# Stores of normalized rows moved from SyncE's to ScalarE's DMA queue, and two parameter loads moved to a later block

## The chip, the cores and the metric

The kernel runs on one core of a Trainium2 chip. The metric is the time of one execution on the device in microseconds (us), as the median of several runs. Engines are named as in the profile: PE is TensorE's matmul (PEld its weight load), DVE is VectorE, ACT is ScalarE, POOL is GpSimd, and SP is SyncE, which here only issues DMAs.

## The reference

Two layers work on x (2708 rows of 256 floats) and a 0/1 adjacency matrix of 2708 x 2708. Each layer is attention and then a mixture of experts, each on a layer-normalized input and each added back to x:

```python
x = x + _L0_gnn_ref(_layernorm(x), adj, L0_gnn_W, L0_gnn_a)
x = x + _L0_ffn_ref(_layernorm(x)[None], L0_ffn_Wg, ...)[0]
x = x + _L1_gnn_ref(_layernorm(x), adj, 1, L1_gnn_W_gcn, ...)
x = x + _L1_ffn_ref(_layernorm(x)[None], L1_ffn_gate_w, ...)[0]
```

The change lies in layer 1. Its attention is a softmax over neighbours, `h_prime = att @ h`, then elu, a projection and maps with logarithms and hyperbolic functions, row by row. Its experts (16 of them, two per row) are:

```python
topk_vals, topk_idx = jax.lax.top_k(x @ gate_w + gate_b, 2)
topk_w = jax.nn.softmax(topk_vals, axis=-1)
h = jax.nn.relu(jnp.einsum('bsh,ehf->bsef', x, w1) + b1)      # F = 512
expert_out = jnp.einsum('bsef,efh->bseh', h, w2) + b2
moe = sum over the two chosen experts of topk_w * expert_out
y = x + moe                        # x is the normalized row here
return (y - mean(y)) / sqrt(var(y) + eps) * gamma + beta
```

The normalized row thus has three uses: it is routed, it is the input of its experts, and it is the start value of y.

## The kernel before, in words

**Tiles and stages.** The 2708 rows are 22 tiles: 20 of 128 rows and two of 74. Layer 0 ends at about 670 us. In layer 1 the attention sums run from about 735 to 871 us: 44 matmuls a tile at L1772, from masks that POOL (L1620) and ACT (L1622) widen. When a tile's sum is done, `finish1` (L1975 to L2002) applies elu on ACT and DVE. When a part of tiles is finished (parts are tiles 0-3, 4-5, 6-9, 10-11, 12-15, 16-17, 18-19, 20-21), `points1` (L2029 to L2111) follows: a DVE and ACT chain of small operations, then for each tile the residual sum with x_d (DVE, L2090; the rows come by `fetch_row`, L1633, on SP), the statistics, and finally for each tile `apply_s` on ACT (L2106, the instruction itself is L506), which writes the normalized row to a tile `xr`. Right behind it `experts1.store` (L2107, the DMA is at L1020) writes this row to `sums[0]` in memory as the start value of y. A tile of 74 rows is stored in two pieces, so there are 24 stores.

**Routing.** Two tiles at a time, `logits1` turns the rows on PE (L515), copies them out on ACT (L610, L613), multiplies with the gate on PE (L520) and takes the logits on DVE (L626). For a group of tiles (0-5, 6-11, 12-17, 18-21), `route1` picks the two best experts (DVE, L648 to L667), ranks rows within experts on PE (L680 to L690), numbers them on DVE (L710 to L746), and POOL scatters the rows to `rows_d`, sorted by expert (L753, two indirect DMAs a tile). After groups 1, 2 and 3 `plan` (L862 to L952) decides which expert each block of 128 sorted rows has: PE L908 (`number_ps`), PE L921 (`where_ps`), ACT L925 (`where`, read by SP into registers at L827), DVE L933, L935 and L937, PE L943 (`bias_ps`), ACT L948. After group 1 (tiles 6-11, counted from 0) blocks 0 to 7 are planned, after group 2 blocks 8 to 19, after group 3 the rest. In the text below "group 2" and "rank 2" belong to tiles 12-17, "group 3" and "rank 3" to tiles 18-21.

**Blocks.** For each of the 45 blocks SP loads both weights of its expert (L834 `w1`, L838 `w2`, 512 KB each) into one of four rooms, so block b waits for the room of block b - 4, and fetches the 128 rows (L850). PE turns them (L515, called turn(b) below), ACT copies them out (L1108), PE multiplies with `w1` (L972, 16 matmuls, hid(b)), ACT applies relu (L976, four), PE multiplies with `w2` (L987 and L990, out(b)), DVE scales (L994, L996), and POOL adds the result to `sums` in memory (L1001). After the last block the sums are read back (L1528), normalized, and stored (L2238).

**What sets the order.** The order of instructions on PE, ACT, DVE and SP is the order in which the program records them (`manual_schedule`, L176). It is recorded by a planner, `Clock` (L65 to L121): each piece of work is a generator that yields an engine and an estimated time before each operation, or a mark it has to wait for; the planner always goes on with the piece that can start first on its modelled engines. An estimate that changes therefore shifts the order of all later operations on all four engines. DMAs of SP are not entered in the planner as work of an engine.

**Gamma and beta.** `late_pools` (L2160 to L2172, called at L1945 once the attention is nearly recorded) makes the buffers of the expert stage and loads gamma and beta with two broadcasting DMAs of SP (`broadcast_rows`, L230). Beta is first read by `add_to_x`, from block 20 on. `beside(b)` (L2174) starts side work at given blocks.

Of the kernel before, what the change touches and what calls it, by code (L numbers as in the profile page):

```python
# [22 lines left out]
P = 128  # L23
# [124 lines left out]
def kernel(  # L148
# [25 lines left out]
    nc = tc.nc  # L174

    ctx.enter_context(tc.manual_schedule(engines={ET.PE, ET.Activation, ET.DVE, ET.SP}))  # L176
    N, D = x.shape
# [50 lines left out]
    def broadcast_rows(name, src, offset, n, queue=nc.gpsimd, pool=const):  # L228
        tl = pool.tile([P, n], F32, name=name)
        queue.dma_start(  # L230
            tl, bass.AP(tensor=src.tensor, offset=src.offset + offset, ap=[[0, P], [1, n]])
        )
        return tl
# [32 lines left out]
    def xr0_tile():  # L266
        return lasting.tile([P, RW], F32, name="xr", bufs=5)
# [14 lines left out]
    def parts_of_rows(r):  # L282

        return [(0, r)] if r == P else [(0, 64), (64, r)]
# [78 lines left out]
    def stat(n, dtype=F32):  # L363

        count[0] += 1
        cols, bufs = next(of for of in STATS if n <= of[0])
        return sm.tile([P, cols], dtype, name=f"stat{count[0]}", tag=f"stat{cols}",
                       bufs=bufs)[:, :n]
# [45 lines left out]
    def rsqrt_steps(v, o=None):  # L414

        yield SMALL
        shifted = ts(v.bitcast(I32), 1, OP.logical_shift_right, dtype=I32)
        yield SMALL
        y = ts(shifted, -1.0, OP.mult, float(0x5F3759DF), OP.add, dtype=I32).bitcast(F32)
        yield SMALL  # L420
        r = tt(v, y, OP.mult)
        yield SMALL
        r = tt(r, y, OP.mult)
        yield SMALL
        h = sts(r, -10.0 / 3.0, OP.add, r, OP.mult)
        yield SMALL
        y = sts(h, 5.0, OP.add, y, OP.mult)
        c = 0.375
        yield SMALL
        h = sts(v, -0.5 * c ** 3, OP.mult, y, OP.mult)  # L430
        yield SMALL
        h = tt(h, y, OP.mult)
        yield SMALL
        return sts(h, 1.5 * c, OP.add, y, OP.mult, o)
# [361 lines left out]
    class Experts:  # L796
# [217 lines left out]
            self.sum_hidden(b, ht, ps)  # L1014
            self.add(b, self.scaled(b, ps, w))

        def store(self, t, r, src):

            for lo, hi in parts_of_rows(r):
                ins = nc.sync.dma_start(self.sums[0][t * P + lo:t * P + hi, :], src[lo:hi])  # L1020
                for _, other in self.adds[0]:
                    tc.declare_no_dep(ins.ins, other, reason="other tokens' rows")

# [604 lines left out]
    def xr_tile():  # L1628
        return side.tile([P, RW], F32, name="xr1", bufs=13)

    def fetch_row(tl, src, t, r):
        for lo, hi in parts_of_rows(r):
            nc.sync.dma_start(tl[lo:hi], src[t * P + lo:t * P + hi, :])  # L1633
# [167 lines left out]
    last = pairs[AHEAD - 1]  # L1801
# [44 lines left out]
    for part in range(2):  # L1846
        for t in range(FIRST + part, LAST, 2):
            for i in range(2):
# [6 lines left out]
    router1 = Router(1, E1, groups1, wg1, bg1, side)  # L1855
    router1.fill()
    sums1 = [sums_d(f"sums1_{k}", zero=k == 1) for k in range(2)]
    experts1 = Experts(1, router1, L1_ffn_w1, L1_ffn_b1, L1_ffn_w2, AF.Relu, sums1,
                       ("wide", "wide", "acc"), lambda b: xr_tile(),
                       lambda: side.tile([P, D], F32, name="lo", bufs=2).rearrange(  # L1860
                           "p (c n) -> p c n", n=P),
                       lambda: w1x[:, 1, :], SURE1, DEEP)
# [166 lines left out]
    def points1(part):  # L2029

        lo, n = part[0][0], len(part)
        hi = lo + n
        xq, xp_slots, x_at = [], [], [Mark() for _ in range(n // 2)]

        def fetch_x():
            for k in range(0, n, 2):
                xp_slots.append((yield from xps.get()))
                for t, r in part[k:k + 2]:
                    xq.append(xr0_tile())
                    fetch_row(xq[-1][:, :D], x_d, t, r)  # L2040
                clock.moved(x_at[k // 2], 0.9, 2.0)

        sq = emb_sq[:, lo:hi]
        v = stat(2 * n)
        yield SMALL
        nc.vector.tensor_scalar(v[:, :n], sq, MIN_NORM * MIN_NORM, None, op0=OP.max)
        yield SMALL
        nc.vector.tensor_scalar(v[:, n:], sq, 1.0, None, op0=OP.add)
        y = yield from rsqrt_steps(v)
        yield SMALL  # L2050
        roots = tt(v, y, OP.mult)
        yield SMALL
        u = tt(roots[:, :n], roots[:, n:], OP.add)
        log = yield from half_log(u)
        yield SMALL
        clock.start(fetch_x())
        inward = sts(log, 0.5 * LEAST, OP.max, y[:, :n], OP.mult)

        for q, (t, r) in enumerate(part):
            yield "ACT", 0.5  # L2060
            nc.scalar.activation(emb[:r, t, 1:], emb[:r, t, 1:], AF.Tanh, scale=inward[:r, q:q + 1])
            yield "ACT", 0.7
            nc.scalar.activation(square[:r, 1:], emb[:r, t, 1:], AF.Square,
                                 scale=0.5, bias=half[:r], accum_out=sig_sq[:r, t:t + 1])

        y = yield from rsqrt_steps(sig_sq[:, lo:hi])
        yield SMALL
        s_n, e = tt(sig_sq[:, lo:hi], y, OP.mult), stat(n)
        yield "ACT", 0.22
        nc.scalar.activation(e, s_n, AF.Exp)  # L2070
        yield SMALL
        ie = recip(e)
        yield SMALL
        sinh = tt(e, ie, OP.subtract)
        by = common[:, lo:hi]
        yield SMALL
        nc.vector.scalar_tensor_tensor(by, sinh, 0.25, y, op0=OP.mult, op1=OP.mult)
        yield SMALL
        cosh = tt(e, ie, OP.add)
        yield SMALL  # L2080
        ratio = recip(by)
        yield SMALL
        ratio = sts(cosh, 0.5, OP.mult, ratio, OP.mult)
        yield SMALL
        nc.vector.tensor_scalar(emb[:, lo:hi, 0], ratio, -1.0, None, op0=OP.add)
        for q, (t, r) in enumerate(part):
            if q % 2 == 0:
                yield x_at[q // 2]
            yield "DVE", 0.5
            nc.vector.scalar_tensor_tensor(x1[:r, t, :], emb[:r, t, :], by[:r, q:q + 1], xq[q][:r, :D],  # L2090
                                           op0=OP.mult, op1=OP.add)
            yield "DVE", 0.62
            ln_f1.stats(x1[:r, t, :], t, r)
            if q % 2:
                clock.set(xp_slots[q // 2])
        dev = ln_f1.rstd[:, lo:hi]
        yield SMALL
        var = ts(ln_f1.mv[:, lo:hi, 1], LN_EPS, OP.add)
        yield from rsqrt_steps(var, dev)
        yield SMALL  # L2100
        shift = ln_f1.shift(part)
        for q, (t, r) in enumerate(part):
            xr_slots[t] = yield from xrs.get()
            router1.rows[t] = xr_tile()
            yield "ACT", 0.6
            ln_f1.apply_s(router1.rows[t][:r, :D], x1[:r, t, :], t, r, shift[:, q:q + 1])  # L2106
            experts1.store(t, r, router1.rows[t][:r, :D])  # L2107
            if q % 2:
                clock.start(logits1(part[q - 1:q + 1], taken_at[t - 1]), urgency(part))
        if hi == group_of(part)[-1][0] + 1:  # L2110
            clock.start(route1(group_of(part)), urgency(part))  # L2111
# [46 lines left out]
    experts1_scope, last = ExitStack(), {}  # L2158

    def late_pools():  # L2160
        last["pool"] = ctx.enter_context(tc.tile_pool(name="gamma_beta", bufs=1))
        for name, src in (("gamma", L1_ffn_gamma), ("beta", L1_ffn_beta)):
            last[name] = broadcast_rows(name, src, 0, D, nc.sync, last["pool"])
        experts1.pool = experts1_scope.enter_context(tc.tile_pool(name="experts1", bufs=1))
        room = experts1.pool.tile([P, 4 * D * 2], F32, name="room2")
        experts1.add_room(2, room[:, :1024], room[:, 1024:])
        for k in range(3, DEEP):
            room = mask_flat.bitcast(F32)[:, 2 * T * D + (k - 3) * 2048:][:, :2048]
            experts1.add_room(k, room[:, :1024], room[:, 1024:])
        last["numbers"] = experts1.pool.tile([P, (T - LATE) * P], F32, name="numbers")  # L2170
        last["marks"] = experts1.pool.tile([P, KEEP, (T - LATE) * P], F32R, name="marks")
        last["kept"] = experts1.pool.tile([P, KEEP, 2, D], F32R, name="kept")  # L2172

    def beside(b):  # L2174
        if b == 10:
            clock.start(number_rows(), 3)
        if 20 <= b < 20 + T:
            clock.start(add_to_x(*tiles[b - 20]), 3)

# [22 lines left out]
    def number_rows():  # L2202
        yield "POOL", 2.0
        nc.gpsimd.iota(last["numbers"], pattern=[[1, (T - LATE) * P]], base=LATE * P,
                       channel_multiplier=0, allow_small_or_imprecise_dtypes=True)
# [295 lines left out]
```

## Time and profile before

| what | value |
|---|---|
| median of 3 runs | 1139.43 us (1137.65 to 1140.55) |
| the profiled execution's own time | 1135.28 us |
| its span, first to last instruction | 1133.6 us |
| mean granted clock of TensorE | 0.961 |
| PE busy | 1038.0 us, 92% of the span |
| DVE, ACT, POOL busy | 48%, 51%, 33% |
| L506 in layer 1, one | 0.585 us |
| L1020 in layer 1: 24 issues on SP, one | 0.319 to 0.547 us, median 0.322 |
| gamma and beta (L230) on SP | at 871.28 and 871.68, 0.35 and 0.42 us |

Times in the profile count from the span's start. A group's row gives its line, engine, operation, output tile and input tiles; a bracket behind a row of the timeline gives the idle time of the engine before it and what released it. The name "SPq" stands for SP's queue of instructions that issue DMAs. "issue" and "remote" as releaser mean that the engine waited for nothing that the profile shows. The busy share is also given in 40 equal slices of the span, one digit each, in tenths.

### The profile page before, as it was taken

How to read it: one execution, taken by the hardware profiler on the slowest of the kernel's cores; microseconds unless marked ns; L12 is line 12 of the kernel's file. 1: busy time of each engine (PE TensorE's matmuls, PEld its weight loads, DVE VectorE, ACT ScalarE, POOL GpSimd, SP SyncE). 2: the span in 40 equal slices, each digit the busy share in tenths (PEclk: the TensorE clock that was granted, in tenths of full speed). 3: DMA queues.
4: the chain of work that ended last, by engine and by line, in shares of the span. 5: the costliest groups of instructions: out<-in, count | busy, mean ns of one | idle time of the engine just before them, and what ended most of it. 6: DMA issues, size and time to landing. Idle time of an engine off the chain costs nothing. (4 is left out here: it accounts for less than half of the span.)

```text
span 1133.6 us, 21472 instructions
## 1 busy us (share of the span) xinstructions
PE 1038.0 (92%) x6707; PEld 921.6 (81%) x6707; DVE 542.4 (48%) x2210; ACT 576.4 (51%) x1602; POOL 368.5 (33%) x425
## 2 busy tenths in 40 slices
PE   5999999998989999999999999898985967999994
PEld 3788888887879999998999854898984856999882
DVE  7778888887421111101110347577865553122257
ACT  4866667664524444444444346545653633544454
POOL 7531112111242222112213361352534155434350
PEclk9999999999999999999999999997996788999997
DMA  9965454431889999999899959401114656785893
GB/s 289 282 248 177 137 176 152 170 95 55 306 252 283 331 323 321 325 305 319 257 312 331 356 155 279 160 1 51 53 61 130 179 138 144 162 203 105 227 292 129
DMA packets 161862, 234.38 MB, mean 207 GB/s; under 512 B 10891, under 2 KB 137798, under 8 KB 159032
## 3 DMA queue, kind: packets, MB, share of 16 engines
q1 hardware_dynamic: 143356, 209.90, 57.0%
q0 software_dynamic: 18384, 23.03, 10.6%
q8 instruction: 56, 0.92, 0.3%
q14 instruction: 66, 0.54, 0.2%
HBM read 205.54 MB, written 54.59 MB: 229 GB/s over the span
## 5 line engine op out<-in xcount | busy, mean ns | idle before, releaser
L996 DVE TENSOR_SCALAR yo<-out_ps,w 128x256 f32<-128x256 f32 x89 | 43.0, 483 | 383.3 <-PE out_ps L990 376.2
L1346 PE MATMUL att_ps<-g_all,z 128*128 128x257 f32 (+3 forms) x968 | 223.6, 383 | 0.0
L1346 PEld LDWEIGHTS att_ps<-g_all,z 128*128 128x128 f32 (+3 forms) x968 | 174.9, 186 | 29.5 <-issue 2.9
L990 PE MATMUL out_ps<-room,ht 128*128 128x256 f32 x840 | 191.4, 380 | 0.0
L972 PEld LDWEIGHTS hid_ps<-xt,room 128*128 128x128 f32 x1504 | 176.9, 194 | 9.3 <-issue 3.7
L972 PE MATMUL hid_ps<-xt,room 128*128 128x128 f32 x1504 | 178.9, 278 | 5.4 <-issue 2.7
L990 PEld LDWEIGHTS out_ps<-room,ht 128*128 128x128 f32 x840 | 155.5, 191 | 20.0
L1332 ACT ACTIVATE zr<-e_bc,minus_one,g_all 128x256 f32<-128x256 f32 (+3 forms) x242 | 130.2, 591 | 44.4 <-DVE z L1335 44.3
L1772 PE MATMUL att_ps<-half,wide_mask 128*128 128x258 f32 (+1 forms) x962 | 131.3, 295 | 14.9 <-issue 8.1
L976 ACT ACTIVATE ht<-hid_ps,w_t 128x128 f32<-128x128 f32 x376 | 128.6, 364 | 30.3 <-PE hid_ps L972 11.7
L1001 POOL DMA_INDIRECT sums<-yo,xg x43 | 66.8, 1554 | 233.8 <-DVE side L964 188.5
L1772 PEld LDWEIGHTS att_ps<-half,wide_mask 128*128 128x128 f32 (+1 forms) x962 | 124.5, 198 | 19.0 <-issue 14.8
L753 POOL DMA_INDIRECT rows_d<-xr,place x88 | 91.8, 1043 | 119.7 <-DVE xr L497 66.4
L1335 DVE SCALAR_TENSOR_TENSOR z<-zr,mask_t 128x256 f32<-128x256 f32 (+3 forms) x242 | 97.8, 424 | 31.1 <-ACT zr L1332 17.4
L976 ACT ACTIVATE ht<-hid_ps,w1x 128x128 f32<-128x128 f32 x180 | 65.1, 366 | 83.5 <-PE hid_ps L972 67.5
L1001 POOL DMA_INDIRECT sums<-yo,xr x42 | 65.7, 1564 | 117.0 <-DMA sums<-yo,xr 40.6
L966 ACT ACTIVATE w<-xg,side 128x1 f32<-128x1 f32 x43 | 12.7, 294 | 165.8 <-DVE side L964 165.8
L1620 POOL CAST wide_mask<-mask_t 128x1408 fp32r<-128x1408 fp8e4 x34 | 47.0, 1387 | 95.8 <-PE att_ps L1772 95.8
L972 PE MATMUL hid_ps<-lo,wide_mask 128*128 128x128 f32 x368 | 51.2, 297 | 3.5 <-ACT lo L1108 3.0
L972 PEld LDWEIGHTS hid_ps<-lo,wide_mask 128*128 128x128 f32 x368 | 49.5, 211 | 5.7 <-ACT lo L1108 3.9
L515 PE MATMUL tr_ps<-ident,xr 128*128 128x128 f32 (+1 forms) x214 | 39.6, 297 | 14.6 <-ACT xr L506 12.9
L515 PEld LDWEIGHTS tr_ps<-ident,xr 128*128 128x128 f32 (+1 forms) x214 | 28.1, 154 | 22.1 <-ACT xr L506 14.2
(334 smaller groups left out, 1442.6 us busy)
## 6 DMA issues: line engine op xcount, KB each, us to landing
room<-in_L_ffn_W_dram SPq DMA_DIRECT2D x94, 1024.0 KB
room<-in_adj_dram SPq DMA_DIRECT2D x20, 1354.0 KB
wide_mask<-in_L_ffn_w_dram SPq DMA_DIRECT2D x46, 512.0 KB
room<-in_L_ffn_w_dram SPq DMA_DIRECT2D x22, 512.0 KB
mask_t<-in_L_ffn_w_dram SPq DMA_DIRECT2D x22, 512.0 KB
rows_d<-nobody SPq DMA_DIRECT2D x1, 7511.0 KB
rows_d<-nobody SPq DMA_DIRECT2D x5, 1295.0 KB
sums<-nobody SPq DMA_DIRECT2D x2, 2944.0 KB
```

The source lines that it names most:

```text
L515: nc.tensor.transpose(ps[:, c, :r], src[:, c * P:(c + 1) * P], ident[:r, :r])
L753: ins = nc.gpsimd.indirect_dma_start(out=self.rows_d[:, :], in_=self.rows[t][:r], in_offset=None, out_offset=bass.IndirectOffsetOnAxis(ap= ...
L972: nc.tensor.matmul(ps[:, :P], w1_b[:, c, f * P:(f + 1) * P], xt[:, c, :], start=(c == 0), stop=(c == DC - 1))
L976: nc.scalar.activation(ht[:, f, :], ps[:, :P], self.func, bias=self.bias[:, f, b:b + 1])
L990: nc.tensor.matmul(ps[:, :D], ht[:, f, :], self.rooms[b % self.deep][1][:, f, :], start=False, stop=(f == self.FC - 1))
L996: nc.vector.tensor_scalar(yo, ps[:, :D], w, None, op0=OP.mult)
L1001: ins = nc.gpsimd.indirect_dma_start(out=self.sums[k][:, :], in_=yo, in_offset=None, out_offset=bass.IndirectOffsetOnAxis(ap=self.rows.pop ...
L1332: nc.scalar.activation(zr[:k, :n], e_bc[:k, lo:lo + n], AF.Relu, bias=minus_one[:k], scale=g_all[:k, j, D + 1:D + 2])
L1335: nc.vector.scalar_tensor_tensor(z[:k, :n], zr[:k, :n], 1.0, mask_t[:k, j // 2, lo:lo + n, j % 2], op0=OP.add, op1=OP.mult)
L1346: nc.tensor.matmul(accs[i][:r, :D + 1], z[:k, q * P:q * P + r], g_all[:k, j, :D + 1], start=(j == 0), stop=(j == LAST))
L1620: nc.gpsimd.tensor_copy(m, src)
L1772: nc.tensor.matmul(accs[i][:, :D + 2], last_masks[i][:k] if late else wide_masks[i, j % 2][:k, j // 2, :], half_k[:k, j, :], start=(j == 0 ...
```

## The change

`store` takes the issuing engine as an argument, with SP as the default, which layer 0 keeps. In `points1`, layer 1's stores are issued by ACT, directly behind the L506 that makes the row, and the planner is told of 0.4 us of ACT for each. The loads of gamma and beta go from `late_pools` to `beside(10)`; the planner records this call while block 10's work is being recorded, and SP stays their issuer.

```diff
-        def store(self, t, r, src):
+        def store(self, t, r, src, queue=nc.sync):
 
             for lo, hi in parts_of_rows(r):
-                ins = nc.sync.dma_start(self.sums[0][t * P + lo:t * P + hi, :], src[lo:hi])
+                ins = queue.dma_start(self.sums[0][t * P + lo:t * P + hi, :], src[lo:hi])
                 for _, other in self.adds[0]:
...
             yield "ACT", 0.6
             ln_f1.apply_s(router1.rows[t][:r, :D], x1[:r, t, :], t, r, shift[:, q:q + 1])
-            experts1.store(t, r, router1.rows[t][:r, :D])
+            yield "ACT", 0.4
+            experts1.store(t, r, router1.rows[t][:r, :D], nc.scalar)
             if q % 2:
                 clock.start(logits1(part[q - 1:q + 1], taken_at[t - 1]), urgency(part))
...
     def late_pools():
         last["pool"] = ctx.enter_context(tc.tile_pool(name="gamma_beta", bufs=1))
-        for name, src in (("gamma", L1_ffn_gamma), ("beta", L1_ffn_beta)):
-            last[name] = broadcast_rows(name, src, 0, D, nc.sync, last["pool"])
...
     def beside(b):
         if b == 10:
             clock.start(number_rows(), 3)
+            for name, src in (("gamma", L1_ffn_gamma), ("beta", L1_ffn_beta)):
+                last[name] = broadcast_rows(name, src, 0, D, nc.sync, last["pool"])
```

## The prediction

> **What bounds the kernel now.** I read the page first, then busy time by stretches, then waits and timelines of the stretch that stood out. By the page TensorE is the bound, with one hole:
>
> ```profile
> PE 1038.0 (92%) x6707; PEld 921.6 (81%) x6707; DVE 542.4 (48%) x2210; ACT 576.4 (51%) x1602; POOL 368.5 (33%) x425
> PE   5999999998989999999999999898985967999994
> PEclk9999999999999999999999999997996788999997
> ```
>
> Slices of 28 us: the hole is where PE shows 5, 9, 6 and the clock 7, 9, 9, 6. Stretches of layer 1 (us, then busy us of PE, PEld, DVE, ACT, POOL, clock, DMA share, GB/s):
>
> ```profile
> 735.00:871.00 136.00, 119.41 (x927) 116.42 (x926) 93.59 (x440) 72.08 (x188) 58.95 (x60) 0.90 0.17 54
> 871.00:960.00 89.00, 62.99 (x407) 56.23 (x405) 48.78 (x305) 34.88 (x111) 36.31 (x39) 0.79 0.60 154
> 960.00:1070.00 110.00, 109.68 (x767) 103.07 (x768) 25.69 (x101) 53.49 (x175) 45.19 (x29) 1.00 0.70 161
> ```
>
> Attention ends at 871; from 960 on PE is full, with 3.84 us a block, and the end follows it. In between PE is idle for 26 of 89 us. Only there can this change win much. PE's idle time there, from its timeline (start, us, what, idle before and its releaser):
>
> ```profile
> 879.78 2.16 PE L515 MATMUL tr_ps<-ident,xr 128*128 128x128 f32 x8 [8.53 <-ACT xr L506]
> 884.67 0.66 PE L515 MATMUL tr_ps<-ident,xr 128*128 128x128 f32 x2 [1.05 <-DVE stat L391]
> ...
> 913.09 0.20 PE L908 MATMUL number_ps<-fresh_bf,tri 58*58 58x32 bf16 x1 [1.66 <-DVE yo L996]
> ...
> 926.35 1.88 PE L943 MATMUL bias_ps<-hot_f,w1x 16*128 16x12 f32 x8 [8.33 <-issue]
> ...
> 943.95 0.27 PE L680 MATMUL rank_ps<-hot,tri 128*128 128x128 bf16 x1 [3.57 <-DVE hot L667]
> ```
>
> SP's own waits from 780 on (total, times, longest) show what the stores cost it:
>
> ```profile
> SPq L1020 <- ACT xr L506: 26.0, 6, 10.7
> SPq L827 <- ACT where L925: 24.4, 2, 22.4
> ```
>
> The stores make SP wait 26.0 us, yet few of these reach PE: no x_d consumer (L2090) waits for its load, and the one visible case is 1.05 us at 884.67, where block 0's turn needs rows whose fetch stood behind two stores (SP: stores 879.75, fetches 881.68).
>
> **What the Trainium skill says.** "DMA: Bandwidth & Descriptors", section Issuing engines are not separate DMA queues: all issuers end on the same 16 DMA engines; issuing from several saves only sequencer time. So no transfer gets faster here. The trace has no DMA issued by ACT to check this. "Perfetto Trace Analysis", section DMA Instruction — HWDGE: the semaphore wait is on the issuing sequencer. SP's 26.0 us agree. "TensorE: Matmul & The Clock Gate", Part 1: half clock after an idle window of about 3.4 us, full again after about as long busy. It agrees: 16 hid matmuls took 3.76 us at clock 0.50 after the 8.53 us hole, 1.95 us at full clock.
>
> **The change, part by part.** *Gamma and beta* leave SP at 871.28 (0.35 + 0.42 us) for a place between two weight loads of about block 13, in the PE-bound stretch: block 1's weights come 0.8 us sooner, and nothing waits for them at that point. Later, 0.8 us of SP lies beside a 3.84 us block; without that cover it would cost 0.8. I take 0.
>
> *SP* loses 24 issues of 0.32 to 0.40 us, 8 to 10 us in all, and the 26.0 us of waiting. Worth on the path: the 1.05 us at 884.67.
>
> *ACT* gains 24 issues. No row of an ACT issue exists; the nearest is SP's L1020, 0.319/0.322/0.547 us. Each also waits until its own L506 (0.585 us) is done, where before four of these ran in 2.07 us, 0.52 apart. Bounds: 0.32 us a store below, 1.0 above; I take 0.55. In the attention stretch 12 stores are 6.6 us beside an ACT busy 72 of 136: hidden, except in the first group. There the fourth L506 ends 1.65 us later (776.17 + 2.08 + 1.65 = 779.9, where PE turned tiles 2 and 3 at 779.09), while six attention matmuls now stand ahead of the first turn and fill 0.8 us of the 4.41 us hole there. Net 0. For tiles 12 to 15 three stores lie between the 8.53 us hole and the last turn: 3 x 0.55 = 1.65 us on the path. (ACT rounds: 0.96 to 3.0.)
>
> *Order.* The recorded order also moves, because a piece of 0.4 us on ACT enters the planner. By the built program PE now turns block 0 before gating tiles 12 to 15; turns and gates tiles 16, 17 directly after hid(0); ranks group 2 after out(0), hid(2) and turn(3), not after out(2); reads where (L925) on ACT ahead of L506 of tiles 18 and 19; and puts bias before most of hid(5), not after hid(6) and out(4). Rank 3 moves from ahead of hid(8) to behind out(8). Worth:
> - hid(0): last turn ends about 883.4, turn(0) 883.8, L1108 after the L610s at 885.0, hid(0) at 885.5 instead of 886.69: the 1.65 us are more than paid by the 1.05 us and by the gates that now stand beside L1108. Gain 1.2.
> - Stage two: rank 2 from 904.67 to about 901.3 (gate of tiles 16, 17 about 3 us sooner). From rank to number is a DVE chain of 8.4 us: number 909.7. Number to where_ps takes 2.9 us, then ACT and DVE about 2 (before: 5.6 us from where_ps to L925, behind L2070 and L506): bias 914.6, 11.7 us sooner. But hid(5), hid(6), out(4) and turns, 6.2 us, are then still owed: equal work at 920.8, 5.5 us ahead; this contains the 1.2.
> - Against it: hot_of was ready at 922.09 and bias began at 926.35; ACT shows 2.19 and 3.94 us "remote" there. Such hesitations without a visible releaser, 6.5 us at this place (4.3 + 2.2), come at the end of each run of 12 scatters (L753: 807 to 824, 852 to 867, 910 to 927). The change keeps the scatters. Recurring in full, they leave 5.5 - 6.5 = -1.0; absent, they also save a second half-clock spell (out 3.62 instead of 1.89, bias 1.88 instead of 1.08: 2.5), 8.0. I take 3.5, the middle.
> - Stage three: out(5) ended at 932.5, hid(8) began at 945.82: 13.3 us, 3.57 of it waiting for rank 3. The new order has no rank there, but a new wait.
>
> *The new wait.* In the built program SP's and ACT's DMAs take one of eight completion semaphores in turn, and each waits for the DMA eight places before it, whichever engine issued that. The first 20 tiles' stores meet only DMAs that are long done: x_d loads that lead L506 by a whole chain, earlier stores, weights of blocks 0, 4 and 5. But tile 20 waits for both weights of block 9, the second of which waits for out(5); tile 21 waits for w2 of block 10, loaded after out(6), and for the fetch of block 8, issued after that. Queued behind them on ACT: two L613 (0.29 us), L1108 of block 8; waiting for these: gate(20, 21) and hid(8), so PE. Price: from out(6)'s end, w2 issue 0.4, fetch issue 1.0 (four in 4.07 us on SP), landing about 2.5 (estimate: w2 of block 1 issued 873.61, four fetches from 881.68 with turn(0) at 884.67, so at most 3.0), L613 and L1108 1.0, gate 0.65: 5.6. PE has out(7) and turns, 2.7 us, so about 2.9 us idle in place of 3.57. Out(6) ends 4 us after out(5): hid(8) at out(5) + 9.6 to 10.5; 2.9 us sooner, less the rank work (1.3) still owed, less 0.6 for number's later cover: 1.0. Bounds: landing 2 to 8 us, so +2 to -4.
>
> **Sum.** 3.5 + 1.0 + 0 = 4.5 us. The profiled execution took 1135.28 (span 1133.6 and 1.7 around it): it would take 1130.8. It was 4.15 below the median of 1139.43; the prediction is for the median: 1134.9.
>
> **Rivals.** *No change:* the hesitation recurs in full, -1.0, and stage three gives its 1.0: 1139.4. For it: three of three scatter runs end in one. Against: PE's waits there were partly ACT's order, which is changed. The same time would result if ACT's issues were too costly to let the chain move, so that the change only shifts work from SP to ACT. *Larger gain:* no hesitation, 8.0, and stage three 1.6 (number's cover holds): 9.6, so 1129.8. *Slower:* ACT stands at the stores of tiles 20 and 21. If w2(10) lands late, because weights of blocks 9 and 10, five fetches and the residual stores share the DMA engines (share 0.69 at 940 to 950), each us is a us of PE. With the hesitation recurring the gain is gone from a landing of about 3.5 us, and at 8 us the loss is 4, with the half clock for hid(8) (3.78 instead of 1.95, as before): 1143.5. Against: 512 KB at the 266 GB/s seen at 890 to 900 are 2 us.
>
> **How the numbers follow.** Forecast (1133 to 1137) 0.47, of which 0.38 lie below the bound of 0.3% (3.4 us), about what a measurement of this kernel can tell from no change; larger gain 0.20, no change 0.21, slower 0.12. Faster 0.58, same 0.30, slower 0.12. The range leaves out part of the larger gain and most of slower: 1129.5 to 1141.5; the likeliest case's own is 1133 to 1137.
>
> **What would show it.** ACT issues of 0.3 to 0.6 us at L1020; no SP wait at L1020 in layer 1; hid(0) by 885.5; rank 2 near 901; bias between 914 and 921; no stall at rank 3 but one of about 3 us before gate(20, 21), released by ACT L613; the 3.84 us steps begin 4 to 5 us sooner. It is wrong if ACT issues cost over 1 us, if a hesitation stands elsewhere in 900 to 930 with full length, or if the stall ahead of hid(8) passes 6 us.

## The result, and the profile after

The changed kernel takes 1150.1 us (median of 6 runs, 1147.47 to 1152.34) against 1140.6 us for the kernel before on the same chip (1137.65 to 1143.71): a ratio of 1.0088, with a 95% interval of 1.0065 to 1.0112. Run again on another chip, beside a second trace of the kernel before, it is 1.0114 (1.0095 to 1.0133). The forecast of 1134.9 us had the wrong sign, and 1150.1 lies above its range.

From the page of the changed kernel (span 1148.7 us), the lines that answer to those shown of before:

```profile
PE 1046.6 (91%) x6707; PEld 928.7 (81%) x6707; DVE 548.0 (48%) x2210; ACT 578.3 (50%) x1602; POOL 368.1 (32%) x425
PE   5999999999989999999999999997785868999993
PEclk9999999999999999999999999998886779999997
```

The hole is wider, the full-clock slices come back later, and PE is busy for longer (1046.6 us against 1038.0) though its instructions are the same 6707, at a mean clock of 0.957 against 0.961. The three stretches of before, in the changed kernel (us, then busy us of PE, PEld, DVE, ACT, POOL, clock, DMA share, GB/s):

```profile
735.00:871.00 136.00, 119.45 (x925) 116.57 (x926) 97.27 (x436) 72.86 (x185) 55.35 (x57) 0.91 0.14 43
871.00:960.00 89.00, 61.55 (x356) 54.78 (x356) 45.79 (x274) 35.23 (x107) 30.71 (x32) 0.76 0.53 147
960.00:1070.00 110.00, 107.59 (x753) 100.42 (x753) 29.37 (x132) 50.66 (x166) 49.42 (x38) 0.98 0.66 149
```

The attention now ends at 881.6, not at 871, so that in the middle stretch PE gets through 356 matmuls where it had 407. Its idle time there, from its timeline, shows what became of the stalls that were forecast to shrink:

```profile
888.12 0.69 PE L515 MATMUL tr_ps<-ident,xr 128*128 128x128 f32 x2 [6.57 <-ACT xr L506]
...
932.27 1.22 PE L972 MATMUL hid_ps<-lo,wide_mask 128*128 128x128 f32 x4 [5.92 <-issue]
935.85 1.88 PE L943 MATMUL bias_ps<-hot_f,w1x 16*128 16x12 f32 x8 [2.36 <-DVE hot_f L933]
...
955.93 0.57 PE L515 MATMUL tr_ps<-ident,xr 74*128 74x74 f32 x4 [1.73 <-ACT xr L506]
957.31 0.77 PE L520 MATMUL gate_ps<-wg,xts 128*74 128x16 f32 x8 [0.81 <-ACT xts L613]
```

The hesitation recurs (5.92), rank 3 no longer stalls PE, and the gate of tiles 20 and 21 does instead. SP's waits of the changed kernel from 780 on: the 26.0 us at L1020 are gone, and fetches now wait for the completion of stores that ACT issues:

```profile
SPq L1633 <- DVE h_all L2090: 54.7, 7, 40.9
SPq L827 <- ACT where L925: 31.2, 1, 31.2
...
SPq L850 <- DMA sums<-xr: 6.9, 3, 4.1
```

ACT's own issues, as one line, are as cheap as the lower bound of the forecast, 0.327 us:

```profile
L1020 ACTq DMA_DIRECT2D sums<-xr x24: 326/327/762, 780.7 to 956.4; - x24
```

**Two traces of one chip.** The first trace of before cannot carry a tally within 5 us: it was 5 us below its median, and PE waits in it from 725 us on for 18.2 us on "issue" (9.6 before bias, 8.1 in the attention sums, 0.5 at hid). On the chip of the last runs this kernel takes 1108.7 us, and its trace (`e17_before`) has none of these. There the two kernels part cleanly. Times are from the start of the attention's long run of sums (734.4 us in the control, 733.4 in the changed kernel), in us:

| mark | control | changed | later by |
|---|---|---|---|
| rank of tiles 0 to 5 | 68.7 | 65.4 | -3.3 |
| rank of tiles 6 to 11 | 108.2 | 116.9 | 8.7 |
| attention ends | 124.6 | 135.8 | 11.2 |
| hid(0) | 140.1 | 150.8 | 10.7 |
| last hid | 338.2 | 349.8 | 11.6 |
| end | 373.7 | 386.3 | 12.6 |

The loss arises in the attention stretch, which the forecast had put at net 0, and 12.0 us of it between the first two ranks. The lead at the first rank is mostly work put off: some 20 sums fewer stand ahead of it, about 2.5 us at the control's rate (54 in 6.75 us). Of these, 6 are done between the ranks and 12 behind the second, where the changed kernel loses another 2.6 us up to the attention's end. PE's timeline of the control between the ranks (start, us, what, idle before):

```profile
803.99 14.94 PE L1772 MATMUL att_ps<-half,wide_mask 128*128 128x258 f32 x122
819.95 5.54 PE L1772 MATMUL att_ps<-half,wide_mask 128*128 128x258 f32 x44 [1.02 <-POOL wide_mask L1620]
825.32 0.60 PE L515 MATMUL tr_ps<-ident,xr 128*128 128x128 f32 x4
827.53 0.99 PE L1772 MATMUL att_ps<-half,wide_mask 128*128 128x258 f32 x6 [1.61 <-POOL wide_mask L1620]
828.36 0.60 PE L515 MATMUL tr_ps<-ident,xr 128*128 128x128 f32 x4
828.72 1.68 PE L1772 MATMUL att_ps<-half,wide_mask 128*128 128x258 f32 x12
830.23 1.85 PE L520 MATMUL gate_ps<-wg,xts 128*128 128x16 f32 x16
...
833.31 0.60 PE L515 MATMUL tr_ps<-ident,xr 128*128 128x128 f32 x4
833.66 1.69 PE L1772 MATMUL att_ps<-half,wide_mask 128*128 128x258 f32 x12
835.19 0.96 PE L520 MATMUL gate_ps<-wg,xts 128*128 128x16 f32 x8
```

and of the changed kernel on that chip (`e18_after`):

```profile
799.61 14.46 PE L1772 MATMUL att_ps<-half,wide_mask 128*128 128x258 f32 x118
815.81 10.81 PE L1772 MATMUL att_ps<-half,wide_mask 128*128 128x258 f32 x88 [1.74 <-DVE stat L396]
830.98 0.44 PE L515 MATMUL tr_ps<-ident,xr 128*128 128x128 f32 x2 [4.35 <-ACT xr L506]
831.99 0.69 PE L515 MATMUL tr_ps<-ident,xr 128*128 128x128 f32 x2 [0.57 <-ACT xr L506]
833.00 0.69 PE L515 MATMUL tr_ps<-ident,xr 128*128 128x128 f32 x2 [0.31 <-ACT xr L506]
834.00 0.69 PE L515 MATMUL tr_ps<-ident,xr 128*128 128x128 f32 x2 [0.32 <-ACT xr L506]
834.98 1.89 PE L520 MATMUL gate_ps<-wg,xts 128*128 128x16 f32 x8 [0.29 <-ACT xts L610]
836.71 1.09 PE L515 MATMUL tr_ps<-ident,xr 128*128 128x128 f32 x4
837.83 3.60 PE L520 MATMUL gate_ps<-wg,xts 128*128 128x16 f32 x16
841.27 8.65 PE L1772 MATMUL att_ps<-half,wide_mask 128*128 128x258 f32 x56
```

The same 12 turning and 24 gating matmuls of tiles 6 to 11 stand in both. In the control they lie between attention sums, one pair of tiles at a time, at full clock: 1.80 + 2.81 = 4.6 us. In the new order 88 sums are recorded ahead of them and the next 56 behind them, so PE has nothing to do while ACT still makes the rows, and from 826.62 to 841.27 it does no sum for 14.65 us. The rows come 1.01 us apart (the starts 830.98, 831.99, 833.00, 834.00), because each waits behind a store. The first of them also comes later than in the control, 97.0 us after the start of the sums against 88.8; 1.35 us of this is a mask widening that ACT now does ahead of it (L1622 at 829.07, L506 at 830.33), and the rest was not traced. And after the hole of 4.35 us PE works at half clock, as the same stretch of both kernels shows (first the changed kernel, then the control; the clock is the third figure from the end):

```profile
829.00:845.00 16.00, 12.49 (x53) 10.66 (x54) 9.82 (x52) 10.87 (x24) 0.00 (x0) 0.58 0.18 58
829.00:845.00 16.00, 15.66 (x148) 15.42 (x147) 11.96 (x63) 11.18 (x27) 3.82 (x8) 1.00 0.16 50
```

From rank to rank the control takes 39.5 us and the changed kernel 51.5. The 12.0 us more are 4.9 of idle time (7.9 against 3.0), 2.7 of slower gates (1.89 + 3.60 against 2.81), 1.8 of slower turns (3.6 against 1.80), about 1.7 of slower sums (56 in 8.65, which took some 7.0 at the control's rate) and about 0.8 for six more sums within the marks. Together 11.9: idle time is less than half of it.

### The profile page after: what moved, and what is told of

The parts are those of the page before. It is cut to its first block, busy times and chain, and to the rows that moved or that the text cites. A ratio compares the mean times of both kernels' runs of the same rounds, so it can differ in the third digit from the quotient of the medians.

```text
span 1148.7 us, 21458 instructions
## 1 busy us (share of the span) xinstructions
PE 1046.6 (91%) x6707; PEld 928.7 (81%) x6707; DVE 548.0 (48%) x2210; ACT 578.3 (50%) x1602; POOL 368.1 (32%) x425
## 5 line engine op out<-in xcount | busy, mean ns | idle before, releaser
L1772 PEld LDWEIGHTS att_ps<-half,wide_mask 128*128 128x128 f32 (+1 forms) x962 | 127.4, 204 | 22.3 <-issue 11.9
L1335 DVE SCALAR_TENSOR_TENSOR z<-zr,mask_t 128x256 f32<-128x256 f32 (+3 forms) x242 | 97.1, 421 | 30.4 <-ACT zr L1332 18.2
L966 ACT ACTIVATE w<-xg,side 128x1 f32<-128x1 f32 x43 | 12.7, 294 | 165.9 <-DVE side L964 165.9
L972 PE MATMUL hid_ps<-lo,wide_mask 128*128 128x128 f32 x368 | 56.3, 317 | 9.1 <-issue 5.9
L972 PEld LDWEIGHTS hid_ps<-lo,wide_mask 128*128 128x128 f32 x368 | 54.5, 230 | 11.2 <-issue 6.5
L515 PE MATMUL tr_ps<-ident,xr 128*128 128x128 f32 (+1 forms) x214 | 39.7, 292 | 12.1 <-ACT xr L506 11.5
L515 PEld LDWEIGHTS tr_ps<-ident,xr 128*128 128x128 f32 (+1 forms) x214 | 27.8, 152 | 20.9 <-ACT xr L506 15.2
```

Of the source, the lines that this page charges most:

```text
L515: nc.tensor.transpose(ps[:, c, :r], src[:, c * P:(c + 1) * P], ident[:r, :r])
L972: nc.tensor.matmul(ps[:, :P], w1_b[:, c, f * P:(f + 1) * P], xt[:, c, :], start=(c == 0), stop=(c == DC - 1))
L1335: nc.vector.scalar_tensor_tensor(z[:k, :n], zr[:k, :n], 1.0, mask_t[:k, j // 2, lo:lo + n, j % 2], op0=OP.add, op1=OP.mult)
L1772: nc.tensor.matmul(accs[i][:, :D + 2], last_masks[i][:k] if late else wide_masks[i, j % 2][:k, j // 2, :], half_k[:k, j, :], start=(j == 0 ...
```

## The experiments

Every ratio is to the kernel before on the same chip, with its 95% interval. Shorthand: the stores are on ACT's queue or not; the planner's entry `yield "ACT", 0.4` is there or not (it alone sets the order of PE, ACT and DVE; without it that order is the one of before); gamma and beta are moved or not. 0.1% is 1.1 us.

**One part at a time.** `e1_qg`: the change without the planner's entry, so with the order of before.

```diff
-            yield "ACT", 0.4
             experts1.store(t, r, router1.rows[t][:r, :D], nc.scalar)
```

> The change without its planner entry: stores on ACT, gamma and beta at block 10, but PE, ACT and DVE keep the order of the kernel before (ACT apart from the stores). Theory 'order' (the 0.4 us entry makes the planner record another order, which puts elu work behind a mask widening on ACT and leaves PE 6 us without an accumulator): most of the loss is gone, 1140 to 1144 us; what is left is the 0.48 us that each row takes longer on ACT, about 1.5 us ahead of block 0. Theory 'ACT issue' (the stores on ACT's queue, their waits for DMAs of SP, and the longer chain): as slow as the change, 1148 to 1152. Theory 'gamma and beta': 1148 to 1152 too.

Measured: 1.0065 (1.0036 to 1.0095). `e2_yg`: the new order and gamma and beta, but the stores stay on SP.

```diff
             yield "ACT", 0.4
-            experts1.store(t, r, router1.rows[t][:r, :D], nc.scalar)
+            experts1.store(t, r, router1.rows[t][:r, :D])
```

> The change with the stores back on SP: planner entry and the moved gamma and beta stay, so PE, ACT and DVE keep the order of the changed kernel. Theory 'order': still slow, 1146 to 1151 us, with PE's wait for an accumulator near 817 us of about 6 us in the trace. Theory 'ACT issue': back at the time before, 1138 to 1142. Theory 'gamma and beta': 1148 to 1152.

Measured: 1.0024 (1.0004 to 1.0044). `e3_g`: gamma and beta alone.

> Gamma and beta alone moved to block 10, all else as before. Theories 'order' and 'ACT issue': within 0.2% of before, 1138.5 to 1142. Theory 'gamma and beta': 1148 to 1152.

Measured: 1.0004 (0.9984 to 1.0025): the step that took them at 0 holds. `e4_qy`: stores and entry, with gamma and beta loaded where they were.

> The change with gamma and beta back in late_pools. Theories 'order' and 'ACT issue': as slow as the change, 1148 to 1152 us. Theory 'gamma and beta': 1138 to 1142.

Measured: 1.0132 (1.0094 to 1.0169). So the new order loses by itself (by an interval that only just leaves out 1) and the stores lose by themselves. `e4_qy` lies 0.4% above the change's 1.0088, but their intervals overlap, and the change itself measured 1.0114 on another chip: that moving gamma and beta helps the other two is not shown. One difference is visible: in `e4_qy` the store of the third row of tiles 12 to 15 is issued 2.0 us after its row is ready (892.10, 894.09), when a load of x_d has landed.

The order's own loss is at the same place as in the pair above. PE's timeline of `e2_yg`, whose stores are on SP:

```profile
822.21 12.64 PE L1772 MATMUL att_ps<-half,wide_mask 128*128 128x258 f32 x88 [6.58 <-DVE stat L396]
834.68 1.38 PE L515 MATMUL tr_ps<-ident,xr 128*128 128x128 f32 x8
836.09 1.06 PE L520 MATMUL gate_ps<-wg,xts 128*128 128x16 f32 x8
839.03 0.93 PE L515 MATMUL tr_ps<-ident,xr 128*128 128x128 f32 x4 [1.87 <-ACT xr L506]
839.99 3.60 PE L520 MATMUL gate_ps<-wg,xts 128*128 128x16 f32 x16
843.42 6.79 PE L1772 MATMUL att_ps<-half,wide_mask 128*128 128x258 f32 x42
```

The wait moves in front of the 88 sums. PE waits there for an accumulator, which DVE's L1993 frees once ACT's L1985 and its followers are done. The long part of it is not the order's: ACT has stood still for 4.64 us with no visible releaser, ahead of the mask widening that precedes L1985. The traces of the pair have no such wait, and there the accumulator costs 1.74. (L2061 and L2063 of four tiles and a widened mask stand ahead of L1985 in the control too, so the elu work behind a mask widening, which the expectation of `e1_qg` gave as the cause, does not tell the orders apart.)

```profile
817.33 1.36 ACT L1622 CAST wide_mask<-mask_t 128x1408 fp32r<-128x1408 fp8e4 x1 [4.64 <-remote]
```

Wait and pause without sums together are 6.58 + 8.57 = 15.2 us here and 1.74 + 14.65 = 16.4 in the changed kernel above, against 3.0 + 4.6 in the control. The block of turns and gates is the order's; the stores add about 1 us to it, by single traces of two chips.

What the two parts do before and after the attention's end, from single traces (they differ by about 3 us for equal work, so only the pattern counts), in us:

| kernels compared | until the attention ends | from there to the end |
|---|---|---|
| order alone: `e2_yg` less `e3_g` | 4.4 | -2.7 |
| stores, old order: `e1_qg` less `e3_g` | 1.7 | 4.4 |
| stores, old order: `e13_q` less `e17_before` | 1.1 | 4.3 |
| stores, new order: change less `e2_yg` | 2.1 | 4.1 |
| order, stores on ACT: `e16_qyg_d4` less `e15_qg_d4` | 10.7 | -1.0 |
| change: `e18_after` less `e17_before` | 11.2 | 1.4 |

The last two rows are of chips whose traces show no waits on "issue" (`e15_qg_d4` and `e16_qyg_d4`, described below, differ by the planner's entry alone). The 4.4 us of the first row are small at least in part because the old order was held up too: PE waits for 3.5 us on "issue" between the first two ranks in `e3_g` and not at all in `e2_yg`. From rank to rank these two take 43.3 and 51.9 us; without the 3.5 us the difference is again 12.0, with the stores on SP. The order thus loses in the attention, with either issuer. In the expert stage the traces show a gain of 1.0 to 2.7, not 4.5, which is within their scatter; and the stores, on ACT, take such a gain back.

**Which stretch of the order?** `e11_ya` and `e7_y12` make the planner's entry for the tiles below 12 and from 12 on, with stores on SP.

```diff
+            if lo < 12:
+                yield "ACT", 0.4
             experts1.store(t, r, router1.rows[t][:r, :D])
```

> The kernel before with the planner's 0.4 us entry for tiles 0 to 11 alone, stores on SP: the attention is recorded as in the changed kernel, the stage after it nearly as before. e7_y12, with the entry from tile 12 on, was 1.0046, e2_yg with both 1.0024. If the accumulator stall of 6 us near 817 us is the price of the entry: 1.003 to 1.006. If the loss of the entry lies after the attention and the attention's stall is paid by the clock that stays up at 780 us: 0.997 to 1.001.

> Stores on SP, gamma and beta moved, and the planner's 0.4 us entry only from tile 12 on, so that the attention keeps the order of before and only the stage after it gets the new one. In e2_yg the attention ended 4.4 us later and the following stage was 2.7 us shorter than in e3_g. Theory 'order': the loss is left out and the gain stays, 0.996 to 0.999 of before. Rival: the gain after the attention came only because the attention was late: 1.000 to 1.003.

Measured: 1.0055 (1.0032 to 1.0077) for the first twelve tiles, with the same stall of 6.08 us ahead of 88 sums; 1.0046 (1.0028 to 1.0064) from tile 12 on (with gamma and beta moved). By its median each half of the order is worse than the whole (1.0024), though the intervals overlap: the orders are different ones, not summands. `e7_y12` lies above the ranges of both of its theories. Where the second half loses its 0.46% its one trace does not show: the end lies 400.3 us after the start of the sums, 4.2 less than in `e3_g`, while its median is higher. `e8_y02` enters 0.2 us, not 0.4.

> Stores on SP, gamma and beta moved, the planner's entry at 0.2 us in place of 0.4, a third recorded order. Theory 'order' (the loss is an accident of which operation the planner records first on ACT ahead of PE's accumulator, not of the size of the entry): anything from 0.996 to 1.006, with the attention's end moved by its own stalls; if the loss grew with the entry, about half of e2_yg's: 1.001.

Measured, with stores on SP and gamma and beta moved: 1.0031 (1.0018 to 1.0044). The loss does not hang on the size of the entry. All four orders that come from an entry are slower than the recorded one of before.

**What do the stores cost?** `e6_fill` leaves everything as before and adds, behind each L506, an ACT copy of the row to a scratch tile that nobody reads.

```diff
             ln_f1.apply_s(router1.rows[t][:r, :D], x1[:r, t, :], t, r, shift[:, q:q + 1])
+            nc.scalar.copy(square[:r, :D - 1], router1.rows[t][:r, :D - 1])
```

> The kernel before, stores on SP, with one more ACT copy of the normalized row into an unused scratch tile behind each of the 22 row operations (255 elements, about 0.5 us each), nothing else moved. It adds work that the result doesn't need. Theory 'ACT time': what e1_qg lost, 1.004 to 1.008 of before. Theory 'shared semaphores': 0.999 to 1.002.

Measured: 1.0002 (0.9985 to 1.0018), though the rows come 0.94 us apart, nearly as with the stores. ACT's time per row alone thus does not make the 0.65% of `e1_qg`. (In the one trace hid(0) came 3.8 us later than in `e3_g`, and the end 0.2 later; what made it up was not found.) `e5_late` and `e12_ylate` issue the stores of a part on ACT behind its last row, without and with the entry.

```diff
-            experts1.store(t, r, router1.rows[t][:r, :D], nc.scalar)
...
+        for t, r in part:
+            experts1.store(t, r, router1.rows[t][:r, :D], nc.scalar)
```

> The stores on ACT without planner entry and with gamma and beta moved, as in e1_qg (1.0065 of before), but each part's stores stand behind its last row and not between its rows; the order of PE, DVE and the rest of ACT is that of before. Theory 'ACT time' (each store between two rows holds the next row back by 0.48 us, because it waits for its own row to be done): the first turn of each part comes in time again, half or more of e1_qg's loss goes, 1.001 to 1.004 of before. Theory 'shared semaphores' (ACT's stores and SP's loads wait for each other): as slow as e1_qg, 1.005 to 1.009.

> The changed kernel with each part's stores on ACT behind its last row and not between the rows; the planner's entries stay where they are, so PE, ACT (stores apart) and DVE keep the changed kernel's order. If stores between rows cost the same in this order as in e1_qg (0.5% of 0.65% went with them), 1.002 to 1.005 against 1.0088 of the changed kernel. If the loss comes from sharing ACT's queue at all: 1.007 to 1.010.

Measured: 1.0016 (0.9989 to 1.0043) and 1.0073 (1.0049 to 1.0096). In the old order the place between the rows seems to matter (1.0065 falls to 1.0016, by intervals that overlap a little); in the new one it hardly does (1.0073 against 1.0088), which fits a loss that lies in the block of turns and gates. `e9_qa` and `e10_qb` put only the stores of the tiles below 12, or from 12 on, on ACT, all else as before.

```diff
+            experts1.store(t, r, router1.rows[t][:r, :D], nc.scalar if t < 12 else nc.sync)
```

> The kernel before, with the stores of tiles 0 to 11 on ACT between the rows and those of tiles 12 to 21 on SP; no planner entry, gamma and beta as before, same order on PE, DVE and ACT. e1_qg, with all stores on ACT, was 1.0065. Theory 'ACT time' (rows of each part 0.48 us apart hold back the turns, in the attention as after it): a third to a half of it, 1.002 to 1.004. Theory 'shared semaphores' (stores and weight loads or row fetches wait for each other, which only the later tiles meet): 0.999 to 1.002.

> The complement of e9_qa: stores of tiles 0 to 11 on SP, of tiles 12 to 21 on ACT between the rows, no planner entry, gamma and beta as before. Theory 'ACT time': the rest of e1_qg's loss, 1.003 to 1.005. Theory 'shared semaphores': all of it, 1.005 to 1.009.

Measured: 1.0009 (0.9994 to 1.0025) and 0.9998 (0.9978 to 1.0018): hardly anything, where the whole had cost 0.65% on another chip, and for the second less than either theory allowed. Either the moved gamma and beta made the difference, or the halves do not add up, or the chips differ.

**Shared completion semaphores?** In the built program the DMAs of SP and ACT take eight semaphores in turn, so each DMA removed or moved shifts which load stands behind which store. `e13_q` moves only the stores; `e14_qg_d2` is `e1_qg` with two tiny loads in gamma's and beta's old place, which restores the turn of `e13_q`; `e15_qg_d4` has four.

```diff
+        for k in range(2):
+            nc.sync.dma_start(spare[:, 8 * k:8 * k + 8], bass.AP(tensor=L1_ffn_gamma.tensor, offset=L1_ffn_gamma.offset, ap=[[0, 1], [1, 8]]))
```

> Only the stores of layer 1's rows go to ScalarE's queue, between the rows; gamma and beta stay where they were and the planner's entry is left out. Theory A (ScalarE's and SyncE's DMAs are issued on the same shared completion semaphores in turn, and the moved gamma and beta shift which load stands behind which store; without them the stores cost what their two halves cost): 0.9990 to 1.0025 of the time before. Theory B (24 stores on ScalarE between the rows cost 0.6% wherever gamma and beta are): 1.0040 to 1.0095.

> As the version with the stores on ScalarE and gamma and beta at block 10 (1.0065), with two tiny loads of eight elements on SyncE's queue where gamma and beta were loaded before, so that every later DMA has the completion semaphore that it has when only the stores are moved. Theory A: like the stores alone, 0.9990 to 1.0030. Theory B: 1.0040 to 1.0095, as without the tiny loads.

> As the last, with four tiny loads instead of two: the turn of the completion semaphores is shifted by four. Theory A: moves by several tenths of a per cent from 1.0065, to either side. Theory B: stays at 1.0040 to 1.0095.

Measured: 1.0044 (1.0027 to 1.0061), 1.0027 (1.0011 to 1.0043), 1.0026 (1.0014 to 1.0038). The first speaks for theory B, the second and third have the sizes of theory A, and the three intervals overlap. The first two have the same turn and the third another: the stores cost 0.3 to 0.4% with both turns, with gamma and beta moved or not. So no effect of the turn shows, which is the core of theory B, though two of its three sizes came out below its range; the turn of `e1_qg` itself was not run on this chip. `e16_qyg_d4`, the changed kernel with four tiny loads:

> The changed kernel with four tiny loads on SyncE's queue where gamma and beta were loaded before. Theory A: moves by several tenths of a per cent from the changed kernel's 1.0088, towards 1.0024 (its order of work with the stores on SyncE) or 1.013 (with gamma and beta as before). Theory B: 1.0065 to 1.0112, as without the tiny loads.

Measured: 1.0147 (1.0123 to 1.0171), above the changed kernel's 1.0088 and, by 0.3%, above its 1.0114 on a chip as quick, whose interval it overlaps. That the turn costs anything in the new order is thus not shown, and the traces of `e16_qyg_d4` and `e18_after` agree within 1 us at the sums and turns shown above.

This run shows something else. It differs from `e15_qg_d4` by the planner's entry alone, and ran beside it on one chip: 1123.4 us against 1112.0. With the stores on ACT in both, the order costs 11.4 us. Their first two ranks (one line further down in these kernels), first in `e15_qg_d4`, where the sums start at 734.62, then in `e16_qyg_d4`, where they start at 734.21:

```profile
803.68 0.26 PE L681 MATMUL rank_ps<-hot,tri 128*128 128x192 bf16 x1
843.35 0.26 PE L681 MATMUL rank_ps<-hot,tri 128*128 128x192 bf16 x1
```

```profile
799.54 0.24 PE L681 MATMUL rank_ps<-hot,tri 128*128 128x192 bf16 x1 [0.25 <-DVE hot L668]
851.08 0.24 PE L681 MATMUL rank_ps<-hot,tri 128*128 128x192 bf16 x1 [0.32 <-DVE hot L668]
```

From rank to rank 39.7 and 51.5 us, as in the pair: the entry alone makes the 12 us, at the same place.

One place where the stores act shows in `e13_q`, at tiles 12 to 15. ACT's timeline:

```profile
868.95 0.60 ACT L506 ACTIVATE xr<-h_all,stat,rstd_f 128x256 f32<-128x256 f32 x1 [0.54 <-ACT xr L506]
870.35 0.33 ACTq L1020 DMA_DIRECT2D sums<-xr  x1
870.85 0.60 ACT L506 ACTIVATE xr<-h_all,stat,rstd_f 128x256 f32<-128x256 f32 x1 [1.30 <-DMA xr<-x_d]
```

The row is ready at 869.55, and the store of it is issued 0.80 later, when a load of x_d that SP issued has landed; the next row stands behind it on ACT. The gate of these tiles begins 5.75 us after the first L506 (872.49 - 866.74), against 2.61 in the control (870.09 - 867.48). That is 3.1 us for three stores, of which hid(0) keeps 2.5. In `e14_qg_d2` and `e15_qg_d4` no store waits there for a load, and hid(0) is 1.7 us later after the attention's end than in the control (17.3 and 17.2 us against 15.6).

**The pair.** `e17_before` is the unchanged kernel, `e18_after` the changed one.

> The kernel before, unchanged, as a control: 0.998 to 1.002 of itself. Its second trace is to tell which of its times up to layer 1's first sums belong to the kernel and which to one execution: if the first trace was a lucky one, layer 1's first long run of sums begins later than 732.4 us or the late stalls are longer than there.

> The changed kernel again, on the same chip as the control, so that two traces of one chip can be laid side by side. Theory C (the loss is the changed order, at the attention's accumulators, plus the stores' own share): 1.0065 to 1.0145, TensorE waits about 6 us for an accumulator and is 4 to 7 us behind the control when the attention ends, the rest lost later. Theory D (the loss is mostly the hesitations with no visible releaser in the expert stage, which differ by execution): the two traces are within 2 us at the attention's end and the loss stands where those hesitations stand.

Measured: 1.0001 (0.9986 to 1.0016) and 1.0114 (1.0095 to 1.0133). Theory C holds in its place: the loss stands where the attention ends. Its size and form differ: 11.2 us there, not 4 to 7, and the wait for an accumulator is only 1.7, with the rest a pause and half clock. Theory D falls on this chip, whose traces have no such hesitations.

## Why the prediction was wrong, by its own steps

**"In the attention stretch 12 stores are 6.6 us beside an ACT busy 72 of 136: hidden ... Net 0."** This step failed, and it decided the sign. The stores themselves are indeed nearly hidden there: in the old order the attention ends 0.4 to 1.1 us later with them (`e13_q`, `e14_qg_d2` and `e15_qg_d4` against the control). What the net of 0 left out is the order. The prediction said that the recorded order moves, but compared the two orders from the attention's end on, and looked at the attention only around the first group; ahead of that the order was put at nothing. There PE's new order waits for ACT's rows at one place and then works at half clock: 11.2 us in the pair, 10.7 by the planner's entry alone on a like chip. A mean share of busy time (72 of 136) could not show that place.

**The first group's hole.** Six sums fill 0.8 us of it, it said, and nothing is gained. The stall moved (4.67 us ahead of these sums, 4.43 ahead of the turn before), but PE was back at full clock by 783.9, where the control still needed 7.91 us for 44 sums at 786: the rank came 3.3 us sooner. But about 2.5 us of that are some 20 sums that the new order does later, so that the gain that was not counted is below 1 us.

**ACT's price, 0.55 us a store.** The mechanism was right and the size nearly: 0.327 us to issue and 0.41 to wait for its own row, rows 1.01 us apart where they were 0.52. Three stores ahead of tiles 12 to 15 were put at 1.65 us on the path to hid(0); two traces give 1.7, and a third 2.5, because one store stood 0.8 at a load's semaphore, where the prediction had only "DMAs that are long done". All 24 stores between the rows cost 0.3 to 0.7% (3 to 7 us); the 1.7 at hid(0) is the largest part that was found.

**Order, stage two and three.** Rank 2, forecast 3.4 us sooner relative to the attention's end, is so: 30.2 us after it in the changed kernel and 33.7 in the control. The gate of tiles 20 and 21 was put at 2.9 us of waiting in place of rank 3's stall; the pair shows 0.47 + 1.73 + 0.80 = 3.0. But rank 2's lead is spent before hid(8): PE's idle time from the first turn's hole to 940 us, the hole itself left out, is 8.4 us in the control and 8.2 in the changed kernel, made of other waits. In the change, the forecast gain of 4.5 after the attention became a loss of 1.4; with the stores left on SP the traces show a gain of 2.7, which is no more than their scatter.

**SP freed, gamma and beta.** SP's 26.0 us of waiting vanish, as forecast. The 1.05 us that this was to bring at block 0's turn is not seen: in the pair that turn waits 0.62 us for its rows, in the control 0.52. Gamma and beta cost nothing (1.0004), as forecast.

**The slower rival** had the right sign with the wrong cause: it put the loss at the stores of tiles 20 and 21. There the stall has the forecast length. Its sum also has a slip: with the hesitation at -1.0 and stage three at +1.0 for a landing of 2.5 us, the gain is gone at 2.5 us, not at 3.5.

**What stays open:** why both halves of the stores cost 0.1% and 0.0% on one chip and the whole 0.4% on another; where the stores lose the rest of their 3 to 7 us; what delays the first rows of tiles 6 to 9 in the new order; where `e7_y12` loses. No version with the stores on ACT, and no order made by the entry, was quicker than the kernel before.

## What to carry to other kernels

Where a planner records the order of all engines, an entry for a small operation is a change of that order everywhere: compare the built orders over the whole stretch, not only where the operation stands, and look for work that lay between other work and is now in one block. A hole is priced with what follows it: here 4.4 us of waiting brought some 6 us more in work at half clock. Moving a DMA to the engine that makes its data frees the old queue, but makes that engine wait for its own result and for the DMA's semaphore: it may pay to put such issues behind the last row that another engine waits for (here 1.0016 in place of 1.0065 in the old order, but 1.0073 in the new one).

## What the runs showed that was not expected

**The clock after a hole.** "TensorE: Matmul & The Clock Gate", Part 1, of the Trainium skill says that about 3.4 us of sustained work bring the full rate back. Here it took longer, and not equally long. After the hole of 4.35 us the changed kernel is at a clock of 0.50 until 845, though PE is busy without a break from 838 on. After the first group's hole of 4.43 us the control is at 0.50 until about 791.5, 12.7 us after its first turn. The trace that the prediction was made from has the same, with PE busy all the time (us, then PE; the clock is the third figure from the end):

```profile
780.00:790.00 10.00, 10.00 (x49) 10.00 (x49) 3.55 (x22) 5.90 (x13) 0.00 (x0) 0.51 0.01 2
```

In `e5_late`, with the same PE order and the same hole, the clock is back at 1.00 at 784, 3.3 us after the first turn (780.73), and the first rank comes 4.4 us sooner than in the control. What decides between the two, no run here shows; a single trace can differ from the next by this much.

**DVE behind POOL.** A residual sum (median 0.47 us) took 3.52 in the control, until two casts of POOL were over (826.10 to 828.77). It happens twice more in the pair, with 2.36 us in the control and 3.42 in the changed kernel, and each time the sum ends 0.3 us behind POOL's cast (it begins, by the profile, 0.5 to 0.7 us ahead of it). "SBUF — State Buffer", Terms, has it that the loser of the port pair which the two share is blocked for the full instruction; the traces agree in so far as the sum waits for the cast's end. DVE's line, then POOL's:

```profile
825.54 3.52 DVE L2090 SCALAR_TENSOR_TENSOR h_all<-h_all,common,xr 128x256 f32<-128x256 f32 x1
```

```profile
826.10 2.67 POOL L1620 CAST wide_mask<-mask_t 128x1408 fp32r<-128x1408 fp8e4 x2
```

**Hesitations belong to the chip.** The waits on "issue", 18.2 us of PE from 725 us on, which the prediction weighed as a risk of this place in the code, are absent from the six traces of the last two chips (`e13_q` to `e18_after`), and present in all fourteen of the others. On the chip of the pair the unchanged kernel took 1108.7 us at a granted clock of 0.970 where it had taken 1139.4 with 0.961. A part of the forecast was argued from a stall that another chip does not have.
